# Deformable convolution by bands: a third buffer of y weights, an earlier place for the x loads and the statistics, one buffer of picked pixels, and one copy handed to a DMA

## The chip, the core and the metric

The kernel runs on one core of a Trainium2 chip. The metric is the device time of one launch in microseconds (us); the value before is the median of three runs. The engines are named as in the profile: PE (TensorE; its weight loads are PEld), DVE (VectorE), ACT (ScalarE), POOL (GpSimd) and SP (SyncE, which here only issues DMAs). A name such as L862 is a line of the kernel before.

## The reference, cut to what matters

The input x holds 8 images of 128 channels and 64x64 pixels in float32. Two layers follow each other, each with a group norm ahead of it and a residual sum behind it. Only the first is touched by the change:

```python
x = x + conv0(gn(x), off_w, off_b, w, b, gamma, beta)      # deformable conv, layer 0
x = x + conv1(gn(x), gate_w, gate_b, gate_bias, expert_w, expert_b, shared_w, shared_b)

# conv0: a plain 3x3 conv gives 27 maps; 18 are offsets, 9 go through a sigmoid and are masks
om   = conv3x3(x, off_w) + off_b
off, mask = om[:, :18], sigmoid(om[:, 18:])
# each of the 9 taps of each output pixel samples x at its own place plus its offset
py, px = row - 1 + ky + off_y, column - 1 + kx + off_x
val  = bilinear(x, py, px) * mask                          # zero outside of the image
y    = einsum("bckhw,ock->bohw", val, w) + b
yn   = (y - mean) * rsqrt(var + 1e-5)                      # over batch, rows and columns
out  = relu(yn * gamma + beta)
```

Layer 1 routes every image to two of four experts (3x3 convs whose weights are mixed per image) and adds a shared conv.

## The kernel before, in words

**Bands.** `dense()` computes layer 0 of one launch. The work is cut into 64 bands: 8 images, each of NB=8 bands of 8 output rows. Band number g is image b, band j. The loop `for g in range(len(bands) + 1)` does two things for PE in each turn: it samples band g, and it does the conv of band g-1. "The iteration of band 4" is the turn with j=4.

**Sampling as a matmul.** Bilinear sampling of offsets that stay under a small reach is written as a product of a tent function in x and one in y. Two tables lie in DRAM for each image: `tabx` with distances in x, `taby` with finished tent values in y times the mask. Per band, `load_x(g)` (L744, POOL, two DMAs of 576 KB with everything replicated over the partitions) fills one of three buffers `x_wts`, and `load_y(g, k)` (L725, POOL, eight DMAs, 720 KB in all) fills one of two buffers `y_wts[g % 2]`. `spread(g)` turns x distances into tents: absolute values on ACT (L763, L766) and a clip on DVE (L769), each in two halves. `weights(n)` (L846, DVE) multiplies x and y weights of a fifth of a band (a group q) to `s`, a pool of four buffers; it is called AHEAD=3 groups ahead, so the fourth and fifth group of a band are made while its first ones are sampled. `sample(n)` multiplies pixels by `s` on PE into `pq` (L862, three PSUM buffers), and ACT copies `pq` to `samples` (L872).

**Pixels.** `pick(g)` (L778, DVE, two copies) takes the pixels of a band out of the padded image `pad` into one of two buffers `picked`; `pixels(g)` transposes them on PE (L807) and copies the result to `xt` on ACT (L810). Odd tiles are made from the even ones by `share(g, piece, move)` (L821), four copies of 32x896 elements, by turns on DVE (0.62 us) and ACT (0.94 us). Only the first two bands make odd tiles in another way, through `picked_odd`.

**Conv.** `conv(g)` is nine taps on PE (L911) into the one PSUM buffer `py`, with a copy to `y` on ACT (L919, two buffers) and a store of y to DRAM on SP (`yd`, L921). The last band of an image has two such convs, of five and four rows.

**What lies beside the taps.** `conv` is a generator that yields after each tap, and the loop issues other work at each of the nine parts (0 to 8):

```python
if odd == 0 and part == 2:
    load_x(g + 3, nc.gpsimd)
...
if odd == 0 and part in (2, 3, 4, 6):
    piece = {2: 0, 3: 2, 4: 1, 6: 3}[part]
    share(g + 2, piece, MOVES[piece])
```

Transposes come at parts 0 and 1, the ACT halves of `spread(g + 2)` at 1 and 3, its DVE halves at 5 and 7, `pick(g + 3)` at part 4. `load_y(g + 2, k)` is issued while groups 2 and 3 of band g are sampled; its buffer `y_wts[g % 2]` is the one that band g's own multiplications read. All engines run their queues in the order in which the code issues; nothing reorders it (`manual_schedule`). DMAs of POOL go through eight lanes: an issue waits for the DMA eight before it on its queue; so on SP.

**Making the tables.** While image b is sampled, the tables of image b+2 are made (b+1 and b at the start). `statistics(b)` is eight bn_stats on DVE (L303, 0.62 us each), which run in the iteration of band 5. `tables(b)` is a long generator that `tick()` moves on a step at a time, three steps a tap. It holds: group means and variances (`pm` L318, `pv` L328 on PE), normalisation of `pad` (L343 on ACT, L347 on DVE), sums and differences of rows called combos (L421, L423 on DVE, 1.2 us each), three blocks of matmuls of the offset conv ("pairs", L456, about 2.8 us each), mixes of their results (`om`), a trip of `om` through DRAM (L523 to L568), `nudge` (L614), distances (L618, L629), tents (ACT L639, L643), masks (DVE `work` L676) and the stores of the tables (L594, L666). `pause(n)` lets n ticks pass; a `BLOCK` makes the generator wait for one of the parts 2, 3, 4, 7 or 8.

**The start.** The tables of image 0 are made before the first band, with loads and stores in small pieces on several queues; `quad_weights()` (in the iteration of band 4 of image 0) derives weights for the combos of later images.

Of the kernel before, what the change touches and what calls it, by code (L numbers as in the profile page):

```python
# [8 lines left out]
F32 = mybir.dt.float32  # L9
# [56 lines left out]
def deform_moe_conv(  # L66
# [113 lines left out]
    def dense():  # L180

        with ExitStack() as st:
# [11 lines left out]
            picked = [a1.tile([P, EVEN, 2, Q, Q], F32, name=f"picked{i}") for i in range(2)]  # L194
            picked_odd = a1.tile([P, EVEN - 1, 2, Q, Q], F32, name="picked_odd")
# [62 lines left out]
            y_wts = [a1.tile([P, T, 3, W, 3], F32, name=f"ywts{i}") for i in range(2)]  # L258
# [50 lines left out]
            def tables(b):  # L309
# [9 lines left out]
                yield from pause(2)  # L319
# [224 lines left out]
                yield from pause(16)  # L544
# [35 lines left out]
                yield from pause((50, 9)[b] if b < 2 else 35)  # L580
# [116 lines left out]
                store_x(0, 2, nc.gpsimd)  # L697
                load_x(0, nc.gpsimd)
# [7 lines left out]
                for k in range(Q):  # L706
                    for h in range(2):
                        load_y(0, k, (nc.sync, nc.gpsimd, nc.scalar, nc.gpsimd)[k % 4], (h,))
                for _ in statistics(1):
                    pass  # L710
                for tiles in ((NCOL, NCOL + 1), (0, 3), (3, 9), (9, NCOL)):
                    spread(0, tiles)
                store_x(2, 6, nc.gpsimd)
                store_x(6, NROW, nc.sync)
                store_y(0, NR, slice(4 * T, H))


            def load_y(g, k, engine, halves=(0, 1)):

                if g >= len(bands):  # L720
                    return
                b, j = bands[g]
                first, last = max(0, k - 2 * REACH), min(T - 1, k)
                n, h = len(halves), halves[0]
                engine.dma_start(  # L725
                    out=y_wts[g % 2][
                        HALF * h + k : HALF * (h + n) : Q, first : last + 1
                    ].rearrange("p r a b c -> p (r a b c)"),
                    in_=bass.AP(
                        tensor=y_table[b].tensor,  # L730
                        offset=y_table[b].offset
                        + (2 * j + h) * T * GROW + (T * k + first) * YSTEP,
                        ap=[[T * GROW, n]] * (n > 1)
                        + [[0, Q], [1, (last + 1 - first) * YSTEP]],
                    ),
                )
# [34 lines left out]
            def pick(g):  # L771

                if g >= len(bands):
                    return
                b, j = bands[g]
                for h in range(2):
                    one = pads[b % 2][:, 2 * T * j + T * h : 2 * T * j + T * h + 1, 0:1]
                    nc.vector.tensor_copy(  # L778
                        picked[g % 2][:, :, h],
                        bass.AP(  # L780
                            tensor=one.tensor, offset=one.offset,
                            ap=[list(one.ap[0]), [Q, EVEN], [1, Q], [W, Q]],
                        ),
                    )


            def pixels(g, turn_odd=False):
# [4 lines left out]
                if turn_odd:  # L792
                    for side in range(2):
                        nc.vector.tensor_copy(
                            picked_odd[:, :, :, T * side : T * side + T].rearrange(
                                "p c h x y -> p c h (x y)"
                            ),
                            picked[g % 2][
                                :, 1 - side : EVEN - side, :, T * side : T * side + T
                            ].rearrange("p c h x y -> p c h (x y)"),  # L800
                        )
                for c0 in range(0, NCOL if turn_odd else EVEN, 4):
                    n = min(4, NCOL - c0)
                    pt = ps_c.tile([P, 4, P], F32, name="pt", tag="pc")
                    for c in range(c0, c0 + n):
                        one = picked[g % 2][:, c] if c < EVEN else picked_odd[:, c - EVEN]
# [19 lines left out]
            MOVES = (nc.vector.tensor_copy, nc.scalar.copy) * 2  # L826
# [4 lines left out]
            def weights(n, engine=nc.vector):  # L831
# [6 lines left out]
                by_y = y_wts[g % 2].rearrange("p r y w x -> p (r y) w x")  # L838
# [6 lines left out]
                for at, c, w, k in parts:  # L845
                    engine.tensor_tensor(  # L846
# [118 lines left out]
            for n in range(AHEAD):  # L965
                weights(n, nc.vector if n < AHEAD - 1 else nc.gpsimd)
# [7 lines left out]
            PIXELS, BLOCKS, SPREAD = (0, 1), (2, 3, 4, 7, 8), (1, 3, 5, 7)  # L974

# [24 lines left out]
            for g in range(len(bands) + 1):  # L1000
                b, j = bands[g] if g < len(bands) else (B, 0)
                if j == NB - 3:
                    means_of = statistics(b + 2)
# [3 lines left out]
                for q in range(NGR):  # L1007
                    if g < len(bands):
# [3 lines left out]
                        if q in (2, 3):  # L1012
                            for k in range(T * (q - 2), T * (q - 1)):
                                load_y(g + 2, k, nc.gpsimd)
# [10 lines left out]
                for done, _ in enumerate(taps):  # L1025
# [3 lines left out]
                    if odd == 0 and part == 2:  # L1029
                        load_x(g + 3, nc.gpsimd)  # L1030
                    if odd == 0 and part in SPREAD:
# [5 lines left out]
                    if odd == 0 and part in (2, 3, 4, 6):  # L1037
                        piece = {2: 0, 3: 2, 4: 1, 6: 3}[part]
                        share(g + 2, piece, MOVES[piece])
                    if odd == 0 and j == NB - 3 and part in (0, 1, 2, 4):  # L1040
                        for _ in range(2):
                            next(means_of, None)
                    if odd == 0 and j == NB - 3 and part == 7 and b + 2 < B:
# [17 lines left out]
                if g == 0:  # L1061
                    for piece in range(4):
                        share(2, piece, MOVES[piece])
                    load_x(3, nc.gpsimd)
                    pick(3)
# [4 lines left out]
                if g == 4:  # L1070
# [604 lines left out]
```

## Time and profile before

| what | value |
|---|---|
| median of 3 runs | 1471.72 us (1462.86 to 1475.43) |
| the profiled execution | 1472.76 us, its span 1471.0 us |
| mean granted TensorE clock | 0.96 |
| up to the first sampling matmul | 0 to 71.3 us |
| layer 0, bands of images 0 to 7 | 71.3 to about 1089 us |
| image 0 (windows between first sample copies) | 163.31 us |
| images 1 and 2 | 119.94 and 125.09 us |
| image 6 | 116.19 us |
| layer 1 | about 1089 to 1471 us |

The windows between first sample copies begin at ACT's first copy of `samples` of the image. The busy shares are means over stages of different kind. The stage of the change is the loop over the bands, and a band's length there is set by the queue that ends last before PE's next sampling group. Images 6 and 7 have no tables to make beside them; image 0 has those of image 1 and part of those of image 2. In a line of the timeline the first number is the start, the second the length, xN the number of instructions drawn together, and the bracket is the idle time before it with what ended it.

### The profile page before, as it was taken

How to read it: one execution, taken by the hardware profiler on the slowest of the kernel's cores; microseconds unless marked ns; L12 is line 12 of the kernel's file. 1: busy time of each engine (PE TensorE's matmuls, PEld its weight loads, DVE VectorE, ACT ScalarE, POOL GpSimd, SP SyncE). 2: the span in 40 equal slices, each digit the busy share in tenths (PEclk: the TensorE clock that was granted, in tenths of full speed). 3: DMA queues.
4: the chain of work that ended last, by engine and by line, in shares of the span. 5: the costliest groups of instructions: out<-in, count | busy, mean ns of one | idle time of the engine just before them, and what ended most of it. 6: DMA issues, size and time to landing. Idle time of an engine off the chain costs nothing.

```text
span 1471.0 us, 21219 instructions
## 1 busy us (share of the span) xinstructions
PE 1300.3 (88%) x7561; PEld 740.1 (50%) x7561; DVE 1064.9 (72%) x2113; ACT 902.7 (61%) x1183; POOL 448.5 (30%) x755
## 2 busy tenths in 40 slices
PE   4169779989989998998998999989975999999998
PEld 1144446555655665664565566556642444444443
DVE  5657687689668868967875896756628877878882
ACT  2365766887787688689777868977723333231320
POOL 6353232343343343343343334344212101011000
PEclk9579989999999999999999999999997999999999
DMA  4485755976887598598778778777618544565411
GB/s 147 106 184 122 164 131 133 208 180 140 182 184 181 129 211 186 126 189 182 171 145 174 179 168 170 174 194 181 175 32 243 140 120 135 149 171 158 114 44 60
DMA packets 146342, 227.33 MB, mean 155 GB/s; under 512 B 100574, under 2 KB 103802, under 8 KB 135986
## 3 DMA queue, kind: packets, MB, share of 16 engines
q0 software_dynamic: 79472, 137.50, 44.6%
q1 hardware_dynamic: 66618, 87.97, 20.4%
q8 instruction: 62, 1.02, 0.3%
q14 instruction: 54, 0.44, 0.1%
q10 hardware_dynamic: 136, 0.41, 0.1%
HBM read 180.23 MB, written 45.35 MB: 153 GB/s over the span
## 4 chain that ended last, share of the span: by engine, by line
PE 46%; DMA 16%; DVE 15%; issue 10%; ACT 9%; POOL 3%; SPq 1%; DVEq 0%; ACTq 0%; POOLq 0%
PE py L911 16%; PE pc L1587 14%; PE pq L862 10%; DMA ywts<-taby 5%; DMA xwts<-tabx 4%; DVE s L846 3%; PE pt L807 2%; PE pc L456 2%; DVE combo L423 2%; ACT xwts L763 2%; DVE stats L303 2%; POOL ywts L725 2%; DVE xwts L769 2%; DVE combo L421 1%; DMA pad<-in_x_dram 1%
## 5 line engine op out<-in xcount | busy, mean ns | idle before, releaser
L911 PE MATMUL py<-samples,dw_sb 128*128 128x512 f32 (+3 forms) x1296 | 553.4, 561 | 7.2 <-ACT y L919 5.4
L725 POOL DMA_DIRECT2D ywts<-taby x512 | 296.6, 600 | 527.3 <-DVE s L846 440.9
L862 PE MATMUL pq<-s,xt 64*128 64x144 f32 (+1 forms) x3840 | 294.1, 307 | 90.8 <-DVE s L846 50.6
L862 PEld LDWEIGHTS pq<-s,xt 64*128 64x128 f32 x3840 | 264.5, 195 | 136.0 <-ACT samples L872 55.3
L911 PEld LDWEIGHTS py<-samples,dw_sb 128*128 128x128 f32 x1296 | 228.2, 189 | 206.7 <-issue 178.1
L872 ACT COPY samples<-pq 128x864 f32<-128x864 f32 (+1 forms) x320 | 282.5, 972 | 53.0 <-PE pq L862 52.1
L846 DVE TENSOR_TENSOR s<-xwts,ywts 128x72 f32<-128x72 f32 (+1 forms) x447 | 199.5, 500 | 68.6 <-PE pq L862 59.2
L1587 PE MATMUL pc<-v,u 128*128 128x512 f32 x384 | 174.2, 600 | 6.3 <-DVE v L1494 6.3
L1587 PE MATMUL pc<-v,wmix 128*128 128x512 f32 x384 | 173.2, 596 | 0.0
L763 ACT ACTIVATE xwts<-xwts,place 128x1152 f32<-128x1152 f32 (+3 forms) x132 | 153.0, 1163 | 23.4 <-DMA xwts<-tabx 21.5
L821 DVE COPY xt<-xt 32x896 f32<-32x896 f32 x126 | 78.5, 623 | 114.2 <-ACT xt L810 113.2
L1565 ACT ACTIVATE t<-pc,bmix 128x512 f32<-128x512 f32 x32 | 22.0, 687 | 187.5 <-PE pc L1587 99.1
L769 DVE TENSOR_SCALAR xwts<-xwts 128x1152 f32<-128x1152 f32 (+2 forms) x128 | 92.9, 755 | 39.9 <-ACT xwts L763 26.3
L821 ACT COPY xt<-xt 32x896 f32<-32x896 f32 x126 | 118.0, 936 | 2.4
L1587 PEld LDWEIGHTS pc<-v,u 128*128 128x128 f32 x384 | 71.8, 191 | 93.0 <-issue 83.1
L1587 PEld LDWEIGHTS pc<-v,wmix 128*128 128x128 f32 x384 | 72.0, 189 | 90.8 <-issue 88.9
L810 ACT COPY xt<-pt 128x512 f32<-128x512 f32 (+1 forms) x130 | 76.1, 586 | 62.2 <-PE pt L807 60.5
L807 PEld LDWEIGHTS pt<-ident,picked 128*128 128x128 f32 x512 | 60.2, 142 | 76.5 <-ACT xt L810 39.0
L744 POOL DMA_DIRECT2D xwts<-tabx x128 | 79.1, 630 | 52.0 <-DMA ywts<-taby 20.5
L807 PE MATMUL pt<-ident,picked 128*128 128x128 f32 x512 | 79.8, 279 | 5.3 <-ACT xt L810 2.9
L919 ACT ACTIVATE y<-py,db_sb 128x512 f32<-128x512 f32 (+3 forms) x72 | 45.7, 635 | 57.3 <-PE py L911 50.0
L778 DVE COPY picked<-pad 128x512 f32<-128x512 f32 x128 | 72.1, 605 | 1.5 <-PE pt L807 0.8
(205 smaller groups left out, 1154.0 us busy)
## 6 DMA issues: line engine op xcount, KB each, us to landing
xwts<-tabx POOLq DMA_DIRECT2D x128, 576.0 KB, 9.4
pad<-in_x_dram SPq DMA_DIRECT2D x36, 512.0 KB
ywts<-taby POOLq DMA_DIRECT2D x126, 144.0 KB, 7.9
out_dram<-yo SPq DMA_DIRECT2D x32, 512.0 KB
ywts<-taby POOLq DMA_DIRECT2D x126, 108.0 KB, 7.6
yd<-y SPq DMA_DIRECT2D x48, 256.0 KB
ywts<-taby POOLq DMA_DIRECT2D x128, 72.0 KB, 7.2
pad<-yd SPq DMA_DIRECT2D x16, 512.0 KB
```

Source lines behind the costliest of these rows:

```text
L725: engine.dma_start(out=y_wts[g % 2][HALF * h + k : HALF * (h + n) : Q, first : last + 1].rearrange("p r a b c -> p (r a b c)"), in_=bass.A ...
L744: engine.dma_start(out=x_wts[g % 3][HALF * h : HALF * h + HALF], in_=bass.AP(tensor=x_table[b].tensor, offset=x_table[b].offset + (2 * j + ...
L763: nc.scalar.activation(some, some, AF.Abs, bias=columns[side])
L769: nc.vector.tensor_scalar(some, some, -1.0, 0.0, ALU.add, ALU.min)
L807: nc.tensor.transpose(pt[:, c - c0], one.rearrange("p h x y -> p (h x y)"), ident)
L810: nc.scalar.copy(xts[g][:, c0 : c0 + n], pt[:, 0:n])
L821: move(out=xts[g][rows, EVEN:].rearrange("p c n -> p (c n)"), in_=xts[g][rows, 1 - side : EVEN - side].rearrange("p c n -> p (c n)"),)
L846: engine.tensor_tensor(s[:, :, 3 * at : 3 * (at + k)].rearrange("p m (c x) -> p m c x", x=3), by_x[:, :, c : c + k], by_y[:, :, w : w + k] ...
L862: nc.tensor.matmul(by_m[:, h, :, at : at + k], lhsT=xts[g][rows, c // 2 + EVEN * (c % 2)], rhs=s[rows, :, at : at + k], start=True, stop=True,
L872: nc.scalar.copy(bass.AP(tensor=one.tensor, offset=one.offset + first, ap=[list(one.ap[0]), [M * PLANE, 2], [PLANE, M], [WB + 1, 3], [1, w ...
L911: nc.tensor.matmul(py, lhsT=dw_sb[:, 3 * (2 - yy) + 2 - xx], rhs=samples[g % 2][:, m : m + 3 * n - 2 : 3, xx, 1 : W + 1], start=(i == 0), ...
L1587: nc.tensor.matmul(pc, lhsT=us[j][:, kx], rhs=vs[g][:, rows, kx : kx + W], start=(kx == 0), stop=(kx == 2),)
```

## The change

1. `y_wts` has three buffers. `load_y(g + 3)` is issued at parts 7 and 8 of iteration g (four DMAs each), behind `load_x(g + 3)` at part 2. It is no longer issued between sampling groups.
2. `picked` is one buffer; `picked_odd` lies in the third buffer of x weights.
3. `statistics(b + 2)` begins in the iteration of band 4 (one bn_stats at each of parts 5 to 8) and ends in band 5 at parts 0 and 1. `tables(b + 2)` begins at part 4 of band 5 instead of part 7 (part 7 as before in image 0), with a pause of 5 ticks instead of 2 behind `pm` for images from 2 on; for image 1 two pauses are divided differently (8 and 17 instead of 16 and 9).
4. `share`: pieces 0 and 2 are copied by DVE at parts 6 and 8, piece 1 by ACT at part 4, and piece 3 by a DMA from SBUF to SBUF on SP at part 2.
5. At the start, rows 2 and 3 of tabx are stored earlier on POOL, the rest of both tables is stored on SP before `statistics(1)`, the third `weights()` runs on DVE instead of POOL, and the first y loads in the loop are issued for bands 2 and 3 in iteration 0. `quad_weights()` moves from band 4 to band 5 of image 0.

```diff
-            picked = [a1.tile([P, EVEN, 2, Q, Q], F32, name=f"picked{i}") for i in range(2)]
-            picked_odd = a1.tile([P, EVEN - 1, 2, Q, Q], F32, name="picked_odd")
+            picked = a1.tile([P, EVEN, 2, Q, Q], F32, name="picked")
...
-            y_wts = [a1.tile([P, T, 3, W, 3], F32, name=f"ywts{i}") for i in range(2)]
+            picked_odd = x_wts[2][:, 0 : (EVEN - 1) * P].rearrange(
+                "p (c h x y) -> p c h x y", h=2, x=Q, y=Q
+            )
+            y_wts = [a1.tile([P, T, 3, W, 3], F32, name=f"ywts{i}") for i in range(3)]
...
-                yield from pause(2)
+                yield from pause(2 if b < 2 else 5)
...
-                yield from pause(16)
+                yield from pause(8 if b == 1 else 16)
...
-                yield from pause((50, 9)[b] if b < 2 else 35)
+                yield from pause((50, 17)[b] if b < 2 else 35)
...
                 store_x(0, 2, nc.gpsimd)
+                store_x(2, 4, nc.gpsimd)
                 load_x(0, nc.gpsimd)
...
+                store_y(0, NR, slice(4 * T, H))
+                store_x(4, NROW, nc.sync)
                 for _ in statistics(1):
                     pass
                 for tiles in ((NCOL, NCOL + 1), (0, 3), (3, 9), (9, NCOL)):
                     spread(0, tiles)
-                store_x(2, 6, nc.gpsimd)
-                store_x(6, NROW, nc.sync)
-                store_y(0, NR, slice(4 * T, H))
...
-            MOVES = (nc.vector.tensor_copy, nc.scalar.copy) * 2
+            MOVES = (
+                nc.vector.tensor_copy, nc.scalar.copy, nc.vector.tensor_copy, nc.sync.dma_start
+            )
...
-                weights(n, nc.vector if n < AHEAD - 1 else nc.gpsimd)
+                weights(n)
...
+            SHARE = 6, 4, 8, 2
...
-                if j == NB - 3:
+                if j == NB - 4:
                     means_of = statistics(b + 2)
...
-                        if q in (2, 3):
-                            for k in range(T * (q - 2), T * (q - 1)):
-                                load_y(g + 2, k, nc.gpsimd)
+                        if g == 0 and q == 2:
+                            for k in range(Q):
+                                load_y(2, k, nc.gpsimd)
...
+                    if odd == 0 and part > 6:
+                        for k in range(T * (part - 7), T * (part - 6)):
+                            load_y(g + 3, k, nc.gpsimd)
...
-                    if odd == 0 and part in (2, 3, 4, 6):
-                        piece = {2: 0, 3: 2, 4: 1, 6: 3}[part]
+                    if odd == 0 and part in SHARE:
+                        piece = SHARE.index(part)
                         share(g + 2, piece, MOVES[piece])
-                    if odd == 0 and j == NB - 3 and part in (0, 1, 2, 4):
+                    if odd == 0 and j == NB - 4 and part > 4:
+                        next(means_of, None)
+                    if odd == 0 and j == NB - 3 and part < 2:
                         for _ in range(2):
                             next(means_of, None)
-                    if odd == 0 and j == NB - 3 and part == 7 and b + 2 < B:
+                    if odd == 0 and j == NB - 3 and part == (4 if b else 7) and b + 2 < B:
...
                     load_x(3, nc.gpsimd)
+                    for k in range(Q):
+                        load_y(3, k, nc.gpsimd)
...
-                if g == 4:
+                if g == 5:
                     quad_weights()
```

More of the change, by code (lines that the diff above doesn't have):

```diff
@@ L725, in load_y @@
                 engine.dma_start(
-                    out=y_wts[g % 2][
+                    out=y_wts[g % 3][
                         HALF * h + k : HALF * (h + n) : Q, first : last + 1
@@ L778, in pick @@
                     nc.vector.tensor_copy(
-                        picked[g % 2][:, :, h],
+                        picked[:, :, h],
                         bass.AP(
@@ L797, in pixels @@
                             ),
-                            picked[g % 2][
+                            picked[
                                 :, 1 - side : EVEN - side, :, T * side : T * side + T
@@ L805, in pixels @@
                     for c in range(c0, c0 + n):
-                        one = picked[g % 2][:, c] if c < EVEN else picked_odd[:, c - EVEN]
+                        one = picked[:, c] if c < EVEN else picked_odd[:, c - EVEN]
                         nc.tensor.transpose(
@@ L824, in share, with weights @@
                 )
-            MOVES = (nc.vector.tensor_copy, nc.scalar.copy) * 2
+            MOVES = (
+                nc.vector.tensor_copy, nc.scalar.copy, nc.vector.tensor_copy, nc.sync.dma_start
+            )
             def width(q):
                 return GT * T + 2 * (q in (0, NGR - 1))
-            def weights(n, engine=nc.vector):
+            def weights(n):
                 if n >= len(bands) * NGR:
@@ L837, in weights @@
                 by_x = x_wts[g % 3].rearrange("p (c m x) -> p m c x", m=M, x=3)
-                by_y = y_wts[g % 2].rearrange("p r y w x -> p (r y) w x")
+                by_y = y_wts[g % 3].rearrange("p r y w x -> p (r y) w x")
                 main = GT * T * q
@@ L845, in weights @@
                 for at, c, w, k in parts:
-                    engine.tensor_tensor(
+                    nc.vector.tensor_tensor(
                         s[:, :, 3 * at : 3 * (at + k)].rearrange("p m (c x) -> p m c x", x=3),
```

## The prediction

> **What bounds the kernel now.** I read the busy shares first, then the windows band by band, then the waits, last the timeline of TensorE (PE).
>
> ```profile
> PE 1300.3 (88%) x7561; PEld 740.1 (50%) x7561; DVE 1064.9 (72%) x2113; ACT 902.7 (61%) x1183; POOL 448.5 (30%) x755
> ...
> 373.65:389.88 16.23, 16.23 (x116) 11.18 (x116) 11.90 (x25) 13.93 (x17) 6.09 (x10) 1.00 0.63 144
> 389.88:402.99 13.11, 13.11 (x90) 7.87 (x88) 8.08 (x17) 10.60 (x13) 6.14 (x10) 1.00 1.10 220
> 402.99:418.92 15.93, 14.54 (x110) 9.08 (x106) 9.52 (x22) 13.00 (x18) 5.68 (x10) 1.00 0.95 223
> 418.92:435.42 16.50, 15.00 (x86) 9.28 (x86) 11.55 (x26) 14.72 (x21) 5.94 (x10) 0.90 0.70 150
> 435.42:451.44 16.02, 12.84 (x70) 7.22 (x72) 15.10 (x33) 11.79 (x16) 6.42 (x11) 1.00 0.90 210
> ```
>
> PE carries the kernel. The window rows (length, then busy time of PE, weight loads, DVE, ACT and POOL, granted clock, DMA share, GB/s) are bands of image 2; the second is a plain band, 13.11 us and all of it PE. The next three hold the same conv and sampling and take 3 us more each: there the other engines make PE wait. The fourth has clock 0.90 and 15.00 us busy, so PE also ran slower. Layer 1 (about 380 us) is untouched, so everything lies in the first 1089 us.
>
> ```profile
> 420.00 3.27 PE L862 MATMUL pq<-s,xt 64*128 64x144 f32 x24 [2.47 <-ACT samples L872]
> 436.50 1.92 PE L862 MATMUL pq<-s,xt 64*128 64x144 f32 x24 [1.50 <-ACT samples L872]
> 447.44 0.35 PE L318 MATMUL pm<-mv,gsel 128*128 128x1 f32 x2 [0.92 <-DVE mv L306]
> 449.95 0.38 PE L328 MATMUL pv<-e,gsel 128*128 128x1 f32 x2 [1.18 <-DVE e L323]
> 466.84 1.94 PE L862 MATMUL pq<-s,xt 64*128 64x144 f32 x24 [0.86 <-ACT samples L872]
> 484.94 1.87 PE L862 MATMUL pq<-s,xt 64*128 64x144 f32 x24 [1.75 <-DVE s L846]
> 213.62 3.49 PE L862 MATMUL pq<-s,xt 64*128 64x144 f32 x24 [5.62 <-DVE s L846]
> ```
>
> These are the waits of PE in image 2 (and one of image 0); all but pm and pv stand before the fourth sampling group. The bracket is the wait. The same 24 matmuls take 1.9 us after waits up to 1.75 us, and 3.27 and 3.49 after 2.47 and 5.62. So a wait over some 2 us costs about 1.2 us more (mean over the five long waits of images 1 to 5 and this one).
>
> ```profile
> POOL ywts L725 <- DVE s L846: 346.2, 47, 18.3
> DVE xt L821 <- ACT xt L810: 73.8, 30, 4.5
> ACT xwts L763 <- DMA xwts<-tabx: 14.6, 8, 5.2
> ...
> 411.35 1.25 ACT L763 ACTIVATE xwts<-xwts,place 128x1152 f32<-128x1152 f32 x1 [1.86 <-DMA ywts<-taby]
> 440.11 2.47 DVE L303 BATCH_NORM_STATS2 stats<-pad 128x6 f32<-128x512 f32 x4
> ```
>
> In the waits of 236 to 980 us, POOL holds y loads (L725) back for the multiplication (L846), 346 us in 47 waits; POOL is in order, so x loads (L744) come late too. At 411.35 ACT stands 1.86 us for its x weights, and the 2.47 us of PE at 420.00 are what is left of it. In the conv of band 4 the loads are not what is late.
>
> **What the skill says.** "Perfetto Trace Analysis", section "Optimization Strategy", tells to find the gaps of the saturated engine and what blocks it; the seven lines above are that. "DVE: scalar operands, raw-bit mode, write accounting and state across instructions", section 5, says that the DVE's queue is one in-order queue; the trace agrees: an xt copy (L821) that waits for ACT has DVE stand up to 4.5 us. "DMA: Bandwidth & Descriptors", section "Issuing engines are not separate DMA queues", says that DMAs of SP, ACT and POOL share the same 16 engines, so a DMA moved to SP gains issue time only; no row of before isolates this. "TensorE: Matmul & The Clock Gate", section "What's actually happening", puts the drop to a slower clock at about 3.4 us of idleness; here 2.47 us was enough, and the measurement decides.
>
> **The change, part by part.** Let C be the start of a conv on PE. Group 3 of the next sampling could start at C+11.8 in a plain iteration (436.50 less 1.50 less 423.20). Its product s (0.42 us, the first of three) is the first thing that DVE does after its pile for the band, so PE is free about 0.5 us after the pile ends.
>
> *Loads.* y loads no longer wait for s (third buffer), x loads go ahead of them: all 2+8 DMAs of a band stay on POOL (2x0.63+8x0.60=6.1 us of 13). x weights come 4 to 7 us earlier, and ACT has one xt copy less (0.94 us). The wait of band 3's iteration was 3.55, 2.47, 1.24, 3.85, 5.75 in images 1 to 5, mean 3.4, plus 0.95 of slow matmuls: 4.3. ACT's y copy moves up from 418.35 by the 1.86, though one tent step more lies ahead, so 0.6 stays: -3.7.
>
> *Statistics in band 4.* Four bn_stats of 0.62 join that pile. DVE in order: work (tent 2, waits for ACT, ends C+3.7), nudge 0.5, dist_x 1.1 (C+5.4), work of tent 3. ACT gets to that tent after pt copy (C+3.5), three abs (2.6) and L639/L643 (0.76+0.68): C+7.6. Then DVE work 0.7 (8.3), pick 1.1 (9.4), clip L769 0.7 (10.1), four statistics 2.5, two xt copies 1.2, clip 0.7, work 0.7: C+15.2. PE starts at 15.7, a wait of 3.9 where it was 1.5, and over 2 us: +1.2. Together +3.6. From below: +0 if tent 3 came first and statistics lay in DVE's idle time ahead of it.
>
> *pm and pv.* The sums are ready at C+4.1 and asked for after tap 4 (C+5.4); pv after tap 7. Both waits (mean 1.9) go to 0.2: -1.8 (rounded up for the taps behind).
>
> *Tables start earlier* (part 4 of band 5), so combos (L421/L423, 1.2 us each) move up a band. Band 6: shift and four normalisations 2.2, pick 1.1, clip, xt, clip (waits for ACT L763, which stands behind four L343, to C+8.5; ends 9.2), combo, xt, two combos 4.2: C+13.4, PE at 13.9, less 11.6 (466.84 less 0.86 less 454.40): 2.3 instead of 0.86, at the limit for slow matmuls, so +0.6 for half of it: +2.0. Band 7: five combos 6.1 (C+6.7), pick 1.1, clip, om mixes 0.85 (behind pair 0 on PE, C+8.2, and ACT, 8.9), four combos 4.8, clip, two xt copies: C+16.5, PE at 17.0, less 14.5 with the pair: 2.5 instead of 1.05, +1.2 for slow matmuls: +2.6. Band 0 of the next image: pair 2 no longer lies between the two convs, so the y copy (ACT, behind an om and an xt copy) shows: +1.0.
>
> Images 1 to 5 each: -3.7+3.6-1.8+2.0+2.6+1.0=+3.7, five times: **+18.5**.
>
> *Piece 3 of share by a DMA on SP.* 115 KB; the nearest row, a y load of 144 KB, takes 7.9 us to landing, and it has over a band (13 us) until its use. Behind it on SP wait the yd stores (y has two buffers) and the tables' round trip: 0, at worst +0.5 a band in some ten bands.
>
> *One picked buffer.* In a steady band the transposes end at C+3.5 and pick comes after C+7: 0. At the start pick(2) must follow band 1's transposes: L614, at 45.36 before, is 1.7 us later. picked_odd in x_wts[2] is done before x loads come there: 0. The third memset of y weights (2 us on POOL at 6 us) lies under the input loads: 0.
>
> *Start.* +1.7 and about +1.0 for the large taby store among the first loads; the wait of 3.37 at 96.44 goes, as the third s is no longer on POOL ahead of the loads of band 1; one ACT copy -1.0: **-1.7** (bounds -5 and +4).
>
> *Image 0.* The 5.62 ahead of 213.62 goes with its slow matmuls (-7.2), since the combos come behind s; ACT's 7.46 of band 4 is 0.9 shorter; two pairs pushed into the next image and combos that move cost +1.8; quad_weights at band 5 takes what pm and pv give: **-6.3**. Images 6 and 7 have no table work in them: x loads -0.5-1.5, y copy +0.6: **-1.4**.
>
> Sum 18.5-1.7-6.3-1.4=+9.1 on the profiled 1472.8 (span 1471.0 and 1.8 around it): 1481.9; the median lies 1.0 lower than the profiled run, so **1481**. A measurement here tells about 1%, 14.7 us, from no change.
>
> **Rivals.** (a) *The cover holds:* the piles of bands 4, 6 and 7 end no later than before. For it: DVE is busy 11.55 of 16.50 in band 4. Against it: its idle time lies ahead of the pile. Per image -3.7-1.8+1.0=-4.5, five times -22.5, with -9.4: 1440; with two of the three holding half, about 1455. (b) *VectorE's queue becomes the bound, slower:* in bands 4, 6 and 7 s is 1 us later than summed each, as every wait for ACT is handed on in order; it decides once the waits of bands 6 and 7 pass some 2.4 us, as then each has slow matmuls too (+0.9): +3.9 an image, +19.5: 1500. (c) *Transfers were hidden anyway:* band 3's wait stays, because ACT's pile and not the x weights makes it; the wait at 411.35 speaks against it. +3.7 five times: 1499. (d) *The change doesn't do what it says:* POOL waits for its DMA lanes instead of s (35.7 us in 22 waits already), and x comes no earlier: as (c).
>
> **How the numbers follow.** The forecast 0.50, (a) in whole or half 0.22, (b) 0.18, (c) and (d) 0.10. The forecast's own range is 1468 to 1490 (start +-4, band sums +-1.5 an image); a tenth of it lies over 1486, where 1% above begins. The range takes in the half of (a) and (b) up to its number: 1453 to 1502. Faster by over 1%: 0.22, all of (a); slower: 0.28 of (b), (c) and (d) and 0.05 of the forecast, 0.33; within: 0.45.
>
> **What would show it.** Right: POOL's wait on s gone; the band 3 wait under 1 us; pm and pv without waits; the fourth group of band 4 waiting about 4 us on DVE with slow matmuls; 2 to 3 us in bands 6 and 7; the first sample near 74. Wrong: group 3 in bands 4, 6, 7 waiting under 1.5 us (then (a)), a wait in band 3 that stays, or SP's copy holding back a sampling group.

## The result, and the profile after

The changed kernel takes 1507.07 us (median of 4 runs, 1503.19 to 1507.68), the kernel before 1468.41 (4 runs on the same occasion): a ratio of 1.0255, 95% interval 1.0202 to 1.0308. It is slower. The forecast was 1481, with a range of 1453 to 1502. The profiled execution took 1507.33 us (span 1505.5, clock 0.942). First the busy shares, then image 2 from band 2 on and band 0 of image 3, in windows between ACT's first copies of `samples`:

```profile
PE 1324.1 (88%) x7561; PEld 757.6 (50%) x7561; DVE 1065.7 (71%) x2114; ACT 844.1 (56%) x1120; POOL 459.6 (31%) x755
...
399.44:412.55 13.11, 13.11 (x90) 7.87 (x88) 8.12 (x19) 9.65 (x13) 6.76 (x11) 1.00 0.91 209
412.55:426.54 13.99, 13.99 (x104) 8.75 (x102) 9.55 (x22) 12.65 (x19) 6.15 (x10) 1.00 1.05 218
426.54:441.20 14.66, 13.98 (x96) 8.30 (x92) 11.36 (x26) 14.14 (x20) 5.73 (x10) 1.00 1.02 220
441.20:459.02 17.82, 14.02 (x70) 8.44 (x72) 15.43 (x34) 9.81 (x14) 1.14 (x2) 0.90 0.72 165
472.13:494.80 22.67, 18.98 (x138) 11.19 (x136) 20.19 (x30) 10.60 (x14) 8.19 (x15) 0.85 0.62 143
494.80:520.51 25.71, 22.03 (x204) 15.18 (x202) 15.89 (x31) 13.23 (x17) 5.53 (x10) 0.93 0.45 118
```

PE has the same 7561 instructions, but they are busy 23.8 us longer: they ran slower. ACT has 58.6 us less to do, and the kernel is slower all the same. Bands 3 and 4 are the gain (13.99 and 14.66 where 15.93 and 16.50 stood). Bands 5, 7 and 0 are the loss (17.82, 22.67 and 25.71 where 16.02, 15.99 and 20.98 stood), and in these the granted clock is 0.90, 0.85 and 0.93. A part of band 7 is only work moved there: it has 138 matmuls where it had 118, and band 6, of 13.11 us where 14.33 stood, has 90 where it had 110. Bands 0, 6 and 7 before are the first three rows below. (In the prediction the first window row, 373.65 to 389.88, is not a band: band 1 begins at 377.65. None of its sums uses that row.) The last two rows, images 2 to 5 before and after, show how much is slow running and how much is waiting:

```profile
356.67:377.65 20.98, 20.15 (x204) 14.16 (x202) 17.56 (x32) 14.25 (x18) 5.55 (x10) 1.00 0.61 135
451.44:465.77 14.33, 14.33 (x110) 9.09 (x106) 11.50 (x24) 13.33 (x18) 5.98 (x11) 1.00 0.58 131
465.77:481.76 15.99, 15.13 (x118) 8.14 (x116) 14.94 (x23) 11.30 (x16) 5.80 (x10) 1.00 0.77 181
...
356.67:863.18 506.51, 470.43 (x3420) 291.05 (x3418) 391.75 (x780) 398.29 (x513) 191.42 (x324) 0.98 0.79 171
361.50:894.30 532.80, 485.66 (x3420) 302.04 (x3418) 391.93 (x781) 368.71 (x480) 194.93 (x324) 0.95 0.76 170
```

The same 3420 matmuls take 15.2 us longer, and PE stands idle for 47.1 us instead of 36.1. PE's timeline from band 5 of image 2 to band 0 of image 3 has the waits:

```profile
445.00 3.16 PE L866 MATMUL pq<-s,xt 64*128 64x144 f32 x24 [3.94 <-DVE s L850]
...
453.80 0.28 PE L320 MATMUL pm<-mv,gsel 128*128 128x1 f32 x2
456.65 0.28 PE L330 MATMUL pv<-e,gsel 128*128 128x1 f32 x2
...
477.24 3.49 PE L866 MATMUL pq<-s,xt 64*128 64x144 f32 x24 [3.69 <-DVE s L850]
480.66 2.07 PE L915 MATMUL py<-samples,dw_sb 128*128 128x512 f32 x2
498.97 2.55 PE L866 MATMUL pq<-s,xt 64*128 64x144 f32 x24 [2.75 <-DVE s L850]
515.18 4.22 PE L915 MATMUL py<-samples,dw_sb 128*128 128x256 f32 x18 [0.93 <-ACT y L923]
```

There are three waits of 2.75 to 3.94 us, all for s on VectorE, where 1.50, 0.86 and 1.75 were (the last in image 3; band 0 of images 2, 4, 5 and 6 had 0.83 to 0.93). pm and pv have none, as meant. After 3.69 us not only the 24 matmuls of the fourth and fifth group are slow (3.49 against 1.9) but the taps behind them too (2.07 for two where 1.14 is usual). POOL's wait for s ahead of the y loads (346 us) is gone from the list of waits. Ahead of them it now waits for other DMAs, and 62 us of waits for s stand ahead of the x loads:

```profile
POOL ywts L727 <- DMA xwts<-tabx: 120.2, 64, 3.8
POOL ywts L727 <- DMA ywts<-taby: 67.5, 46, 4.0
POOL xwts L746 <- DVE s L850: 62.1, 9, 12.6
```

Where the 34.5 us of the two spans lie (windows from one image's first sample copy to the next's):

| stretch | before | after | moved |
|---|---|---|---|
| start to first sample copy | 73.42 | 76.24 | +2.8 |
| images 0 and 1 | 283.25 | 285.26 | +2.0 |
| images 2 to 5 | 506.51 | 532.80 | +26.3 |
| image 6 | 116.19 | 119.33 | +3.1 |
| image 7 and layer 1 | 491.6 | 491.9 | +0.3 |

### The profile page after: what moved, and what is told of

It reads as the page before. It is cut to its first block, busy times and chain, and to the rows that moved or that the text cites. A ratio compares the mean times of both kernels' runs of the same rounds, so it can differ in the third digit from the quotient of the medians.

```text
span 1505.5 us, 21262 instructions
## 1 busy us (share of the span) xinstructions
PE 1324.1 (88%) x7561; PEld 757.6 (50%) x7561; DVE 1065.7 (71%) x2114; ACT 844.1 (56%) x1120; POOL 459.6 (31%) x755
## 4 chain that ended last, share of the span: by engine, by line
PE 45%; DVE 18%; DMA 13%; issue 11%; ACT 7%; POOL 2%; SPq 2%; DVEq 0%; POOLq 0%; ACTq 0%
PE py L915 18%; PE pq L866 11%; PE pc L1599 9%; PE pc L458 3%; DVE combo L425 3%; PE pt L809 3%; DMA ywts<-taby 2%; DVE s L850 2%; DMA taby<-work 2%; DMA x<-in_x_dram 2%; DVE stats L305 2%; DVE xt L823 2%; ACT xwts L765 2%; DMA yd<-y 2%; DVE xwts L771 1%
## 5 line engine op out<-in xcount | busy, mean ns | idle before, releaser
L915 PE MATMUL py<-samples,dw_sb 128*128 128x512 f32 (+3 forms) x1296 | 563.7, 568 | 9.4 <-ACT y L923 7.6
L727 POOL DMA_DIRECT2D ywts<-taby x512 | 314.3, 637 | 350.1 <-DMA xwts<-tabx 173.6
L866 PE MATMUL pq<-s,xt 64*128 64x144 f32 (+1 forms) x3840 | 307.9, 316 | 109.5 <-DVE s L850 100.8
L866 PEld LDWEIGHTS pq<-s,xt 64*128 64x128 f32 x3840 | 275.7, 202 | 159.1 <-issue 102.9
L850 DVE TENSOR_TENSOR s<-xwts,ywts 128x432 f32<-128x432 f32 (+1 forms) x448 | 198.3, 496 | 36.5 <-PE pq L866 32.9
L746 POOL DMA_DIRECT2D xwts<-tabx x128 | 74.4, 588 | 279.5 <-DVE ystats L996 73.8
L771 DVE TENSOR_SCALAR xwts<-xwts 128x1152 f32<-128x1152 f32 (+2 forms) x128 | 96.0, 750 | 86.6 <-ACT xwts L765 82.6
L809 PEld LDWEIGHTS pt<-ident,picked 128*128 128x128 f32 x512 | 63.8, 149 | 80.2 <-ACT xt L812 39.1
L809 PE MATMUL pt<-ident,picked 128*128 128x128 f32 x512 | 83.1, 287 | 5.3 <-ACT xt L812 2.9
L823 ACT COPY xt<-xt 32x896 f32<-32x896 f32 x63 | 59.1, 938 | 1.5
```

Of the source, the lines that this page charges most:

```text
L727: engine.dma_start(out=y_wts[g % 3][HALF * h + k : HALF * (h + n) : Q, first : last + 1].rearrange("p r a b c -> p (r a b c)"), in_=bass.A ...
L746: engine.dma_start(out=x_wts[g % 3][HALF * h : HALF * h + HALF], in_=bass.AP(tensor=x_table[b].tensor, offset=x_table[b].offset + (2 * j + ...
L771: nc.vector.tensor_scalar(some, some, -1.0, 0.0, ALU.add, ALU.min)
L809: nc.tensor.transpose(pt[:, c - c0], one.rearrange("p h x y -> p (h x y)"), ident)
L823: move(out=xts[g][rows, EVEN:].rearrange("p c n -> p (c n)"), in_=xts[g][rows, 1 - side : EVEN - side].rearrange("p c n -> p (c n)"),)
L850: nc.vector.tensor_tensor(s[:, :, 3 * at : 3 * (at + k)].rearrange("p m (c x) -> p m c x", x=3), by_x[:, :, c : c + k], by_y[:, :, w : w + ...
```

## The experiments

Theory 1 is that work on VectorE which now stands ahead of s makes the waits; theory 2, its rival, that the late copies of `share` and its DMA do. A further pair asks whether the slow matmuls belong to the waits. All times are medians beside the kernel before (1470.5 to 1472.4). Times per image are from one profiled execution of each kernel.

**The change with the statistics and tables where they were** (share still changed):

```diff
-                if j == NB - 4:
+                if j == NB - 3:
                     means_of = statistics(b + 2)
...
-part == (4 if b else 7) and b + 2 < B
+part == 7 and b + 2 < B
...
-                yield from pause(2 if b < 2 else 5)
+                yield from pause(2)
```

with the eight bn_stats at parts 0, 1, 2 and 4 of band 5 again.

> The changed kernel with the statistics and the tables where they were before: bn_stats in band 5 only, tables from part 7 of band 5, pause of 2 behind pm. Loads, share, start as changed. Theory 1 (statistics and combos that stand ahead of s on VectorE make the three long waits of an image): the waits of 3.9, 3.6 and 2.7 us ahead of the fourth group shrink to 2.7 (both xt copies still lie late in the pile of band 4), about 1 and about 1, the slow matmuls behind the last two go, pm and pv cost 2 us again: about 9 us less per image, 1507 to about 1455. Theory 2 (the late xt copies on VectorE and the DMA of share make them): waits stay over 2 us, 1495 to 1507.

Measured 1468.39 (ratio 0.9983, 0.9961 to 1.0006). 38.7 us are undone, but 1455 was expected: theory 1 is not all.

**The kernel before with only these moved**: the same edit the other way round.

> The kernel before with only the statistics and the tables moved as in the change (band 4, part 4 of band 5, pause of 5); two y buffers, old loads, old share, old start. Theory 1: the three long waits with their slow matmuls appear on top of the late x weights of band 3: about +8 us an image, 1500 to 1515. Theory 2: no long waits, pm and pv gone: 1458 to 1470.

Measured 1505.75 (1.0224, 1.0162 to 1.0286): this one part of the change makes a loss of nearly the same size (35 us against 39) when the loads are late too. The waits of bands 5 and 7 that theory 1 names are there; the one of band 0 stays at 1.61 us:

```profile
447.77 2.78 PE L862 MATMUL pq<-s,xt 64*128 64x144 f32 x24 [2.69 <-DVE s L846]
478.54 2.83 PE L862 MATMUL pq<-s,xt 64*128 64x144 f32 x24 [2.21 <-DVE s L846]
```

**Loads and start alone** (with the single buffer of picked pixels): as the first, and share as before.

```diff
-            MOVES = (
-                nc.vector.tensor_copy, nc.scalar.copy, nc.vector.tensor_copy, nc.sync.dma_start
-            )
+            MOVES = (nc.vector.tensor_copy, nc.scalar.copy) * 2
...
-            SHARE = 6, 4, 8, 2
+            SHARE = 2, 4, 3, 6
```

> As the first of these, and share as before too (parts 2, 4, 3, 6; two copies on DVE and two on ACT): only loads, the single buffer of picked pixels and the start are changed. Theory 1: the late x weights of band 3 are gone, the rest is as before: about 4 us less an image than before, start +3: 1445 to 1455. Theory 2: also about 1450, and far from the first kernel of this call; by theory 1 the two differ by 5 us or less.

Measured 1451.83 (0.9851, 0.9793 to 0.991), as expected; but it is 17 us from the first where theory 1 allowed 5. So share costs as well, by its copies or by its DMA. The timeline shows the wait that the loads were to remove (2.47 before):

```profile
414.36 1.93 PE L864 MATMUL pq<-s,xt 64*128 64x144 f32 x24 [0.50 <-ACT samples L874]
```

**Matmuls that fill the waits** of the changed kernel, first too many, then fitted:

```diff
                 by_m = pq[:, :, 0 : M * wide].rearrange("p h (m k) -> p h m k", m=M)
+                b, j = bands[g]
+                fill = {5: 8, 7: 7, 0: 5}.get(j, 0) if q == 3 and 8 < g < 50 else 0
+                for _ in range(fill):
+                    nc.tensor.matmul(
+                        pq[:, 0], lhsT=dw_sb[:, 0],
+                        rhs=dw_sb[:, 0:4].rearrange("p t n -> p (t n)"),
+                        start=True, stop=True,
+                    )
```

> The changed kernel with matmuls that nobody reads ahead of the fourth group where it waits: 8, 7 and 5 of 128x512 (3.6, 3.2 and 2.3 us) in bands 5, 7 and 0 of images 1 to 5 (band 0: 2 to 6), into the same PSUM tile that the real ones then overwrite. The results stay whole. Theory A (a wait of over 2 us makes the matmuls behind it slow, and this is the part that the sum missed): the slow matmuls go, about 6 us an image over five images: 1507 to about 1477. Theory B (they are slow for another reason, such as the operands' traffic): no gain, 1505 to 1510.

Measured 1516.86 (1.0292, 1.0227 to 1.0358): a miss of the design. One such matmul is two instructions of PE and takes 0.89 us, so the fill outlasted the wait. Then with 3, 4 and 3:

> The changed kernel with 3, 4 and 3 matmuls of 128x512 that nobody reads ahead of the fourth group in bands 5, 7 and 0, at the 0.89 us that one takes (two passes): 2.7, 3.6 and 2.7 us, about as long as the wait for s that is left once the PSUM tile is free. In the longer fill the matmuls behind ran at full speed but PE was held 2 to 3 us past s. Theory A (the slow matmuls behind a long wait cost about 6 us an image): 1507 to about 1480. Theory B (the clock costs nothing on the path): 1505 to 1510.

Measured 1477.42 (1.0035, 1.0021 to 1.0049), 29.7 us less than the change, with all its VectorE work unchanged. Its timeline:

```profile
433.65 2.84 PE L864 MATMUL pq<-dw_sb 128*128 128x512 f32 x6 [1.21 <-ACT samples L884]
436.43 1.87 PE L874 MATMUL pq<-s,xt 64*128 64x144 f32 x24
...
463.41 3.70 PE L864 MATMUL pq<-dw_sb 128*128 128x512 f32 x8
467.05 1.87 PE L874 MATMUL pq<-s,xt 64*128 64x144 f32 x24
468.84 1.15 PE L923 MATMUL py<-samples,dw_sb 128*128 128x512 f32 x2
```

The fill stands where the wait was, and the matmuls behind it take 1.87 and 1.15 us instead of 3.16 to 3.49 and 2.07. Theory A holds: an image of 2 to 5 goes from 133.20 to 127.63 us with a granted clock of 1.00, so the slow matmuls cost about 5.6 us an image.

**Piece 3 by the DMA, the other copies in their old places**, on the loads-and-start kernel: MOVES as in the change, SHARE = 2, 4, 3, 2.

> The loads-and-start kernel (1452) with piece 3 of share by the DMA on SP at part 2, and the other pieces where they were before (0 and 2 on DVE at parts 2 and 3, 1 on ACT at part 4). Theory 1 (in the change the place of the DVE copies costs, and the DMA is free): ACT has 0.94 us less a band, the waits that ACT ends in bands 4, 5 and 7 (0.5, 1.5, 0.86) shrink: 1438 to 1448. Theory 2 (the DMA on SP is what costs 17 us between the two kernels, as the stores and the table trips stand behind it): 1460 to 1470.

Measured 1449.12 (0.9851, 0.9825 to 0.9877), 1 us above the range of theory 1 and far from that of theory 2. The 17 us are not the DMA's. This kernel and the first experiment (1468.39) differ only in the parts at which VectorE makes its two copies, so it is their place, behind the masks and combos instead of ahead of them, that costs. The gain is small: ACT's waits go, and VectorE's s is next (1.77 us in band 0 where 0.82 was).

**Four statistics at part 0 of band 4, four at part 0 of band 5**, against **the statistics as in the change**, both on the loads-and-start kernel with the tables as before:

```diff
-                    if odd == 0 and j == NB - 3 and part in (0, 1, 2, 4):
-                        for _ in range(2):
+                    if odd == 0 and (j, part) in ((NB - 4, 0), (NB - 3, 0)):
+                        for _ in range(4):
                             next(means_of, None)
```

> The loads-and-start kernel (1452) with four bn_stats at part 0 of band 4, ahead of the tents' masks, and four at part 0 of band 5; tables at part 7 as before. Theory 1 (it is the place in VectorE's queue that costs, not the work: at part 0 of band 4 VectorE stands idle for 3 us anyway): no longer wait ahead of group 3 in band 5, pm waits no more, pv about as before: -1 us an image, 1444 to 1450. Rival (band 4 has no room for 2.5 us of VectorE wherever they stand): as for the next kernel, 1460 to 1470.

> The loads-and-start kernel (1452) with the statistics as in the change (parts 5 to 8 of band 4, parts 0 and 1 of band 5), tables at part 7 as before. By theory 1 the four bn_stats stand right ahead of s: the wait of group 3 in band 5 goes from 1.5 to about 2.7 (the xt copies are early here, 1.2 us less ahead of s than in the change) with slow matmuls behind it, pm waits no more: +2 us an image, 1455 to 1466, and waits in bands 7 and 0 stay under 1 us. Rival (the statistics themselves cost nothing, the earlier combos do it all): 1444 to 1452.

Measured 1436.64 (0.9773, 0.9751 to 0.9794), faster than either theory had it, and 1453.69 (0.9883, 0.9857 to 0.9909), between the two ranges. The timelines, the early one first:

```profile
428.66 1.91 PE L864 MATMUL pq<-s,xt 64*128 64x144 f32 x24 [1.50 <-ACT samples L874]
438.52 0.28 PE L320 MATMUL pm<-mv,gsel 128*128 128x1 f32 x2
439.73 0.38 PE L330 MATMUL pv<-e,gsel 128*128 128x1 f32 x2
```

```profile
432.67 2.62 PE L864 MATMUL pq<-s,xt 64*128 64x144 f32 x24 [3.88 <-DVE s L848]
```

The same eight instructions are 17 us apart. Ahead of the masks they fill time in which VectorE waits for ACT (1.86 and 1.41 us at that place in the loads-and-start kernel); right ahead of s they are a wait of PE. That wait is 3.88 us where 2.7 was expected, because I took the early xt copies to shorten it; with the tables early as well they do (2.69 us, below). Why they don't here stays open. In the late one this loss and the vanished waits of pm and pv just cancel: images 2 to 5 take 122.90 us, without the move 123.16. The early one is the fastest kernel here, within the noise of two variants of it below.

**Tables from part 4 of band 5 (and the pause of 5), with the early statistics:**

> The kernel with four statistics at part 0 of band 4 (1437), but the tables from part 4 of band 5 and a pause of 5, as in the change. Theory 1: the combos that move ahead of s in bands 6 and 7 make the waits of about 2.5 to 3.6 us in bands 7 and 0, with slow matmuls behind them, and the y copy shows: +5 to +6.5 us an image, 1464 to 1472; the wait of band 5 stays at 1.5. Rival (without the late statistics and late xt copies VectorE has room for the combos): 1437 to 1445.

Measured 1465.72 (0.994, 0.9912 to 0.9967), as theory 1 had it: 29 us for the tables alone, 119.15 to 126.11 us an image in images 2 to 5.

```profile
458.18 2.99 PE L864 MATMUL pq<-s,xt 64*128 64x144 f32 x24 [2.22 <-DVE s L848]
...
477.69 1.86 PE L864 MATMUL pq<-s,xt 64*128 64x144 f32 x24 [1.61 <-DVE s L848]
```

These waits of bands 7 and 0, where 0.85 and 0.82 were, come with the moved combos. The first, of 2.22 us, has slow matmuls behind it, the second, of 1.61, has not. Two waits that were not expected grow too: those for ACT ahead of bands 4 and 5, to 1.59 and 2.16 us from 0.50 and 1.50. What makes these was not followed.

**The change with only share as before:**

> The changed kernel with only share as before (parts 2, 4, 3, 6, two copies on DVE and two on ACT); statistics late and tables early as changed. If late copies cost more beside the early tables, as they lengthen waits that are already over 2 us: 1480 to 1485, the waits ahead of the fourth group about 3.9 in band 5, 2.2 in band 7 and 1.6 in band 0, so share is worth 22 to 27 us here. If share costs its 17 us anywhere: 1488 to 1492 and something else is missing.

Measured 1472.87 (1.0004, 0.9979 to 1.0029), below both ranges. Share is worth 34 us here, more than expected, against 17 with statistics and tables in their old places. The waits are where they were expected, except that band 5 has 2.69 instead of 3.9 (band 0 has 1.6 in half of the images, 2.9 in the others):

```profile
432.86 3.27 PE L864 MATMUL pq<-s,xt 64*128 64x144 f32 x24 [2.69 <-DVE s L848]
463.63 3.32 PE L864 MATMUL pq<-s,xt 64*128 64x144 f32 x24 [2.21 <-DVE s L848]
```

So there is a path of four kernels from before to after. Per image of images 2 to 5, in us, each with the same 3420 matmuls:

| kernel | an image | PE busy | PE idle |
|---|---|---|---|
| before | 126.63 | 117.61 | 9.02 |
| loads and start | 123.16 | 117.36 | 5.81 |
| with statistics and tables | 128.28 | 118.56 | 9.72 |
| with share: the change | 133.20 | 121.42 | 11.78 |

The costs of two parts are not independent, as both lengthen the same three waits. Of the 4.9 us that share adds last, 2.9 are the same matmuls running slower and only 2.1 are longer waits.

In the trace of this kernel a wait of 2.69 us ahead of the fourth group has slow matmuls behind it in image 2 (432.86) and none in image 3 (560.64). The granted clock shows why. Between 200 and 1000 us of every trace here it changes only at points that lie 3.41 us apart; below are the stretches between such points around these two waits, those of image 2 first:

```profile
429.72:433.13 3.41, 0.72 (x12) 0.54 (x10) 3.41 (x6) 3.38 (x6) 0.00 (x0) 1.00 0.50 185
433.13:436.55 3.42, 3.42 (x25) 2.90 (x23) 3.39 (x11) 2.02 (x3) 1.07 (x2) 0.50 0.43 108
556.01:559.43 3.42, 1.95 (x32) 1.73 (x30) 3.42 (x7) 3.36 (x6) 0.00 (x0) 1.00 0.58 158
559.43:562.84 3.41, 2.19 (x25) 1.85 (x26) 3.38 (x9) 3.38 (x5) 1.07 (x2) 1.00 0.22 82
```

In image 2 the wait falls into one stretch, PE is busy for 0.72 of 3.41 us, and the next stretch is granted half the clock. In image 3 a point of change cuts the wait in two, PE is busy for more than half of either stretch, and the clock stays at 1.00 in the second and in the one behind it.

**Two pieces by DMA** (MOVES: DVE, ACT, DMA, DMA; SHARE = 2, 4, 2, 2), on the early-statistics kernel:

> The kernel with four statistics at part 0 of band 4 (1437), and pieces 2 and 3 of share both by DMAs on SP at part 2: one copy less on VectorE (0.62 us) and one less on ACT (0.94 us) in every band. Theory 1 (VectorE and ACT both end just late ahead of the fourth group, so both must have less): the waits of 0.5, 1.5, 0.85 and 0.82 shrink to about 1.2 in all: -2.4 us an image, 1421 to 1430. Rival (the DMAs' traffic or SP's queue takes it back): 1437 to 1445.

Measured 1450.57 (0.9846, 0.9778 to 0.9913): 14 us slower than without, a clear miss. SP's queue in band 4 without the DMAs, then with them, and three waits of the latter:

```profile
424.11 2.17 SPq L596 DMA_DIRECT2D tabx<-combo  x6
426.39 0.96 SPq L283 DMA_DIRECT2D pad<-in_x_dram  x1
```

```profile
422.06 7.90 SPq L596 DMA_DIRECT2D tabx<-combo  x6
430.07 0.40 SPq L283 DMA_DIRECT2D pad<-in_x_dram  x1
...
435.92 1.29 DVE L305 BATCH_NORM_STATS2 stats<-pad 128x6 f32<-128x512 f32 x2 [4.45 <-DMA pad<-in_x_dram]
...
437.75 0.35 PE L320 MATMUL pm<-mv,gsel 128*128 128x1 f32 x2 [1.12 <-DVE mv L308]
441.46 0.59 PE L330 MATMUL pv<-e,gsel 128*128 128x1 f32 x2 [2.37 <-DVE e L325]
```

The six stores of the x table take 7.90 us to issue instead of 2.17, the image load behind them leaves 18.9 us after the band's first sample copy instead of 13.7, statistics wait for it, and pm and pv wait again. With one such DMA a band (1449.12 above) the six stores still take 2.17 us. To tell this from the DMAs' own cost, **the DMAs only outside of bands 2 to 4** (there pieces 2 and 3 by DVE and ACT at part 2):

> The kernel with four statistics at part 0 of band 4 (1437), with pieces 2 and 3 of share by DMAs on SP, but by DVE and ACT in bands 2, 3 and 4, where SP has the image loads and the stores of the x table. If SP's queue was the loss: pm and pv wait as little as without the DMAs, the waits of bands 7 and 0 shrink from 0.85 and 0.82: 1428 to 1436. If the DMAs themselves cost: 1442 to 1450.

Measured 1438.18 (0.9761, 0.9709 to 0.9812). The loss is gone, so it was made by the DMAs of bands 2 to 4, where the stores and image loads stand behind them on SP; those of the other bands cost nothing that shows. But no gain is left either (images 2 to 5: 118.92 us against 119.15). What stretches the issue of the stores was not tested.

**The start**, three kernels: before with only the start's stores and the third s on DVE; before with only one buffer of picked pixels; and the early-statistics kernel with the third memset moved:

```diff
-            for t in y_wts:
+            for t in y_wts[0:2]:
                 nc.gpsimd.memset(t, 0.0)
...
                 if b == 0:
+                    nc.gpsimd.memset(y_wts[2], 0.0)
                     for piece in range(4):
```

> The kernel before with only the start's stores moved (rows 2 and 3 of tabx early on POOL, the rest of both tables on SP ahead of the statistics of image 1) and the third s on VectorE. With this start all kernels so far sampled first at 75.9 to 76.8 us instead of 73.4. If the stores did that, the first sample comes at about 75 to 76 here too; if the single buffer of picked pixels did it (VectorE's L614 went from 45.4 to 48.7), it stays near 73.4. The wait of 3.4 us in band 1 goes. Total 1466 to 1473.

> The kernel before with only the single buffer of picked pixels (picked_odd in the third buffer of x weights). At the start the third pick must wait for the transposes of band 1 and takes the reduction of the offsets and the nudge with it: first sample near 76.5 instead of 73.4, +3 us in all, 1472 to 1476. The rival reading (the stores at the start are it): no change, 1468 to 1472. In the bands no change by either.

> The kernel with four statistics at part 0 of band 4 (1437), with the memset of the third buffer of y weights moved from 10 us, where VectorE's L245 and its statistics stand until POOL's memsets are through (the L245 of 0.2 us takes 5.8 us instead of 3.8), to about 42 us, where VectorE stands idle for 5 us. If the memset was 1.6 us of the late start: first sample at about 75 instead of 76.8, total 1433 to 1437. If not: first sample stays at 76 to 77.

Measured 1464.27 (0.9934, 0.9889 to 0.9979), 1470.48 (0.9999, 0.9976 to 1.0021) and 1436.88 (0.975, 0.9698 to 0.9801); first sample copies at 72.78, 74.30 and 76.05, where before has 73.42 and the early-statistics kernel 76.78. The stores are innocent. One buffer of picked pixels moves L614 from 45.36 to 46.85 and the first sample copy by 0.9 us; 3 us were expected. What is left points to the memset. VectorE and POOL before, then after:

```profile
5.88 3.97 POOL L260 MEMSET ywts<- 128x2304 f32 x2
...
6.04 3.83 DVE L246 TENSOR_SCALAR place<-place 128x2 f32<-128x2 f32 x1
...
10.99 0.37 DVE L306 BATCH_NORM_AGGREGATE mv<-stats 128x2 f32<-128x48 f32 x1
```

```profile
5.86 5.92 POOL L262 MEMSET ywts<- 128x2304 f32 x3
...
6.03 5.78 DVE L245 TENSOR_SCALAR place<-place 128x2 f32<-128x2 f32 x1
...
12.55 0.37 DVE L308 BATCH_NORM_AGGREGATE mv<-stats 128x2 f32<-128x48 f32 x1
```

A small operation of VectorE on 128x2 elements ends just as POOL's memsets do, 2 us later with three than with two, and the first statistics are 1.56 us late. Moved to 43 us the memset frees the small operation (3.83 again), but the pick beside it takes longer, 2.10 us instead of 1.12:

```profile
43.14 2.05 POOL L580 MEMSET ywts<- 128x2304 f32 x1
...
43.94 2.10 DVE L781 COPY picked<-pad 128x512 f32<-128x512 f32 x2 [5.73 <-PE pt L810]
```

L614 only goes from 48.95 to 48.35, and the first sample copy stays above 76, as was expected if the memset were not the cause. It was not hidden in either place. Up to L614 the start then adds up (1.5 us for the pick and 1.6 for the memset, of 3.4), but no run does without the third memset, so its share of the late first sample is argued and not shown.

## Why the prediction was wrong, step by step

**Where PE waits: right in most places.** Late x weights: a wait of 0.6 and -3.7 us an image were forecast; 0.50 to 0.53 and -3.5 measured. The wait is sure, the -3.5 in part luck: two kernels with the late loads of before, those with only the start's stores moved and with only one picked buffer, took 124.09 and 123.29 us an image in images 2 to 5, hardly more than the 123.16 with early loads, and lost their time in other images. That the loads gain 19 us in all is the surer number. pm and pv: right. The statistics' wait: 3.9 forecast, 3.94 measured. Band 7's pile: 2.5 and 2.75. The y copy of band 0: 1.0 and 0.93.

**The step that failed** is the price of slow matmuls. The sum took 1.2+0.6+1.2=3.0 us an image, read from the 24 matmuls behind a wait. The fitted fill shows 5.6: the taps and transposes behind run slow too, most after the wait of band 7 (3.49+2.07 where 1.9+1.14 are usual). The trace of before already shows this for image 0, in the taps after 213.62, and the prediction left them out. In the whole kernel the terms for slow matmuls come to about +8.7 us (3.0 less the 0.95 that goes with the late x weights, five times, less 1.6 in image 0). PE's busy time for the same instructions rose by 23.8. That is 15 of the 25.4 us by which the 34.5 of the spans exceed the 9.1 of the sum; the other 10 are waits.

**The pile of band 6** was 1.1 us short: s at C+14.5 (476.49 less 461.97) instead of C+13.4. VectorE's `shift` waits for POOL, and ACT's normalisation and absolute values, hence VectorE's clip, follow:

```profile
464.22 0.16 DVE L341 SCALAR_TENSOR_TENSOR shift<-gm,scale 128x1 f32<-128x1 f32 x1 [1.25 <-POOL scale L338]
...
470.33 0.76 DVE L771 TENSOR_SCALAR xwts<-xwts 128x1152 f32<-128x1152 f32 x1 [2.92 <-ACT xwts L765]
```

Its wait became 3.55 to 3.69 us instead of 2.3, and its slow matmuls, priced at half, came in full. This is what rival (b) described, a wait for another engine handed on in order, with 1 us as its price and slow matmuls as the point from which it decides. It gave 1500 and was the closest, though of its three bands only band 6's pile was clearly longer than summed.

**Smaller terms.** The start: -1.7 forecast, +2.8 measured; pick was priced about right at L614 (1.7, measured 1.5), but the third memset was put at nothing (hidden under the input loads), and is the likely rest. Images 6 and 7: -1.4 forecast, +3.4 measured, since the second half of a table is made in the first bands of the next image, so that band 0 of image 6 still has it (25.72 us against 21.06). Images 0 and 1 together: -2.6 forecast, +2.0 measured. From the terms: images 2 to 5 +11.5 us beyond the forecast (26.3 less 14.8), start +4.5, image 0 and 1 +4.6, images 6 and 7 +4.8: 25.4, the same sum split by stretches. In images 2 to 5 it is 2.9 us an image, 1.8 of them slow matmuls and 1.1 waits.

**Share was costed at nothing for its DMA, and rightly** (1449 against 1452); but that its DVE copies leave VectorE's idle time for the place just ahead of s was only in the piles and not seen as a choice of its own. It is 4.9 us an image, about as much as statistics and tables (5.1). Rival (a) had the idle time of VectorE ahead of the pile as an argument against itself; the early statistics show that this idle time could have been used. Rivals (c) and (d) fell: loads alone gain 19 us.

## What to carry to other kernels

Where an engine works off one queue in order, as VectorE does here, the place of an instruction can matter more than its length (eight bn_stats moved: 17 us). So put work that is free to move into the time in which that engine waits for another, never between the last wait and the result that the bound engine needs. When a wait of TensorE passes about 2 us, as here, expect slow matmuls behind it, count them for as long as they last and not just in the next group, and look for two edits that lengthen the same wait, since their costs don't add. Take a bundle of edits apart: here the loads gained 19 us, and with the statistics in the right place 34, while the bundle lost 39.

## What the runs showed of the hardware

- In the 15 traces without fills, none of 101 waits of 1.2 to 1.93 us ahead of a fourth group made the 24 matmuls behind it slow (they took 1.9 us). Of 78 waits of 2.0 to 3.39 us 53 did (2.2 to 3.5 us), and of the longer ones all 49 (2.6 us and more). A wait of 2.02 us was enough once (the kernel with one picked buffer), and 3.38 us was not another time (loads and start, 294.50, 1.93 us). Matmuls that nobody reads, put into the wait, prevented it.
- What decides between 2.0 and 3.39 us is in the granted clock of the 17 traces. From 200 to 1000 us, all 206 of its changes lie on points 3.41 us apart, fixed within a run. Of the stretches between two neighbouring points that ran at full clock, the 82 in which PE was idle for 60% or more were all followed by one at half clock, of the 3399 with under 30% none was, and of the 184 between 20 were. So the same wait costs more or less by where it falls on these points. No run moved a wait on purpose to try this.
- VectorE's `place` (L246, on 128x2 elements) took 3.83 and 5.78 us beside two and three memsets of POOL, and ended with them; the operation just ahead of it, on 128x1, took 0.16. A pick beside a memset took 2.10 instead of 1.12 us. I had not expected the two engines to hold each other. The mechanism itself was not tested.
- With two SBUF to SBUF DMAs of 115 KB a band on SP's queue the issue of six stores took 7.90 us instead of 2.17; with one it took 2.17.
